# The residual y turned by VectorE instead of TensorE, and the put-off token pieces at fixed groups

## The chip, the cores and the metric

The kernel runs on one core of one Trainium2 chip. The metric is the device time of one execution, in microseconds. All arithmetic is in fp32 (parts of the score factors in an fp32 form with rounded mantissa). The engines are TensorE (PE in the profile, its weight loads PEld), VectorE (DVE), ScalarE (ACT), GpSimd (POOL) and SyncE (SP), which only issues transfers here.

## The reference

Two layers run on x of four images, 64 x 64 positions of 256 channels each, that is 4096 tokens an image.

```python
# layer 0: attention over all 4096 positions of an image
f = xt @ Wf + bf;  g = xt @ Wg + bg;  v = xt @ Wh + bh          # 32, 32, 128 channels
beta = softmax(einsum('bqd,bkd->bqk', g, f))
y = x + (einsum('bqk,bkd->bqd', beta, v) @ Wo + bo)

# layer 1: triangle attention on y, 8 heads of 32 channels
q, k, v1, v2 = (y @ W).reshape(B, N, N, H, d_k)  for each W
att = softmax(einsum('bilhd,bljhd->biljh', q, k) / sqrt(d_k), axis=2)
out = einsum('biljh,bilhd,bljhd->bijhd', att, v1, v2)
h = layer_norm(y + out.reshape(B, N, N, E) @ Wo)
z = relu(h @ W1 + b1) @ W2 + b2 + h
result = layer_norm(z)
```

The change concerns the term y in `layer_norm(y + out @ Wo)`. Layer 0 leaves y with its channels on the partitions; the layer norm needs tokens on the partitions.

## The kernel before

**Stages.** Images b = 0 to 3 go one after the other. Each has an attention stage (`layer0`, line 498) and a triangle stage (`first_layer1` for image 0, `next_layer1`, line 1491, for the others). The token work of layer 1 (projection by Wo, both layer norms, the two-layer perceptron) of image b runs in pieces inside the triangle stage of image b + 1. After image 3's triangle stage its own tokens are left; they run in `alone` (line 1293). A last check over the sums of the softmaxes (`dens`, from line 1634) chooses whether a safe version must run; with these inputs it doesn't.

**Attention stage.** The queries are cut into 8 blocks of 512 tokens (`qb`), the keys into 8 groups (`k`), so that g = 8 qb + k counts 64 groups. In each group `values` (line 569) issues the scores of the next group, the products with v, and on VectorE the running sum of exponentials `esum`. `parts[k]` is a hand-written list of what group k does for the block before: group 0 the normalization (`norm`: a matmul that sums over partitions gives `den`, then a reciprocal on VectorE), group 1 `output` (y = attention x Wo + x, stored to HBM channel by channel), groups 2 to 7 the projections q, k, v1, v2. In group 7 VectorE also folds `esum` into a tile `part` (tag "hid", one buffer). In image 0, VectorE also turns the x of the later images (`ahead.turn`, L356: eight transposes in 32 x 32 blocks and four stores) in every second group. After the last block comes a passage to the triangle stage (from line 776), in which three tiles with tag "R" stage the last block's results, and in which token tile 0 of the image before is begun and the heads of its tile 1 are made.

**Put-off pieces.** In the triangle stages of images 1 and 2 the second layer norm of the tokens is not done; h and z are stored in HBM (`carried_off`, `summed_off`). The attention stage two images later takes them back: for each of 16 tiles `recall` (load), `settle` (three VectorE operations on 512 elements and the statistics), `rooted`, `polished`, `scaled`, `finish` (two GpSimd multiplications or adds, L1287 and L1288, and the store). Line 761 starts a tile every three groups.

**Triangle stage.** Its 32 steps are pairs of heads by 8 rows. In each step the softmax weights are turned by TensorE into `att` (PSUM) and a copy `attP`; eight products R = att x v2 (128 x 2048, L1007) follow, five or six on VectorE and two or three on GpSimd; TensorE sums each R with v1 as stationary data (`accumulate`, L1017). R has three buffers, GpSimd's Rp two. A period is two steps and the pieces of one token tile. The order inside a period is written out as a list of words (`ORDER`, line 43, for images 1 and 2; `ORDER_LAST` for image 3; `ORDER0` for image 0); each engine executes its own share in that order. R, A, T, S, W, V, t, c are work of the steps: product, accumulate, take, row sums and reciprocals, weights, stationary, turn, copy of the weights. sp and e are scores and exponentials; h0 and h1 are the token heads, sa the statistics on them, m the hidden layer, z the output layer, and so on. The number after a slash says how many periods later the word's work is done.

**The line that matters.** `heads` (line 1114) makes out @ Wo for 256 tokens in PSUM with four matmuls (L1120) and adds y by four TensorE transposes (L1125) that accumulate into the same place:

```python
for cc in range(2):
    nc.tensor.matmul(
        hp[:, n, ts(cc, P)], yc[:, cc, ts(n, P)], ident, start=False, stop=(cc == 1),
        is_transpose=True,
    )
```

`yc` is 256 tokens of y, loaded in `load` (line 1095) with one buffer. The statistics on hp are made by `stats_a` on VectorE in the passages and in `alone`, by ScalarE's `sums_of` in the triangle stages of images 1 and 2, and by `stats` on VectorE in image 3's.

Of the kernel before, what the change touches and what calls it, by code (L numbers as in the profile page):

```python
# [10 lines left out]
F32 = mybir.dt.float32  # L11
# [32 lines left out]
    R03/2 R06/2 t1/2 h0 m0/1 R04/2 c1/2 A03/2 A07/2 R16/2 A04/2 A06/2 R12/2 R10/2 T00/2 fi/2 W0/1 sf/2 R17/2  # L44
    T01/2 A10/2 A12/2 t0/1 R11/2 r0/1 fo/2 R13/2 R15/2 f1/2 h1 m1/1 f0/2 A11/2 c0/1 A16/2 V0/1 R14/2 r1/1 A13/2
    A15/2 R00/1 A17/2 T10/2 A14/2 sp/1 R02/1 sa R05/1 e0/1 R01/1 z0/1 rr/1 T11/2 z1/1 pp/1 e1/1 so/1 A00/1 A05/1
    R07/1 W1/1 A02/1 A01/1 fa S1 ht V1/1 S0 hU hT
# [27 lines left out]
def attention_then_triangle_kernel(  # L75
# [131 lines left out]
    dens = ctile([P, NB, 256 + 16], "dens")  # L207
# [238 lines left out]
    class Late:  # L446
# [5 lines left out]
        def load(self, q):  # L452
            self.y = []
            for cc, tag in enumerate(("A", "yc")):
                t = work.tile([P, 512], F32, tag=tag, name="yb", bufs=1)
                nc.sync.dma_start(out=t, in_=self.io["y"][ts(cc, P), ts(q, 512)])
                self.y.append(t)
            self.used = 0
# [39 lines left out]
    def layer0(b, F, safe, rest, ahead):  # L498
# [8 lines left out]
        io["v1"] = dram.tile([T, C], F32, tag="v1", name="v1d")  # L507
        L = Layer1(b, io, safe)
# [105 lines left out]
        def bounds(qb):  # L614
            for j, (t, op) in enumerate(ends.pop(qb)):
                if not safe:
                    c0 = 256 + 2 * qb + j
                    nc.vector.tensor_reduce(dens[:, b, c0 : c0 + 1], t, AX.X, op)
# [7 lines left out]
        def output(qb):  # L626
            col = ts(qb, QB)
            o = oT.pop(qb)
            for cc in range(2):
                y_ps = pb("y")  # L630
                nc.tensor.matmul(y_ps, wo0_sb[:, 0, ts(cc, P)], o, start=True, stop=True)  # L631
                nc.vector.scalar_tensor_tensor(
                    y(qb, cc), y_ps, bo_sb[:, cc : cc + 1], yT[cc][:, col], ALU.add, ALU.add
                )
                nc.sync.dma_start(out=io["y"][ts(cc, P), col], in_=y(qb, cc))

# [91 lines left out]
        if late:  # L728
            parts[3] = [lambda qb: proj(qb, "k", 0)]
            parts[4] = [lambda qb: proj(qb, "v2", 0)]  # L730
            parts[5] = [proj1_half]
            parts[6] = [lambda qb: proj(qb, "q", 1)]
            parts[7] = [lambda qb: proj(qb, "k", 1)]
        last = NQB - 1
        for r in range(4):
            score(0, r)
        for g in range(8 * NQB):
# [22 lines left out]
            if b > 1:  # L760
                for do, late in ((rest.finish, 7), (rest.scaled, 6), (rest.polished, 5), (rest.rooted, 4), (rest.settle, 3), (rest.recall, 0)):
                    if (g - late) % 3 == 0 and 0 <= g - late < 3 * NP:
                        do(NP * (b - 2) + (g - late) // 3)
# [29 lines left out]
        bounds(last)  # L793
        proj(last, "v2", 0, None, stage[1][:, 0, :], nc.scalar)
# [55 lines left out]
    class Layer1:  # L850
        def __init__(self, b, io, safe):
            self.b, self.io, self.safe = b, io, safe

            self.aT = dram.tile([C, 2, N // 2, N], F32, tag="aT", name="aT")
            io["a"] = self.aT
            self.S, self.v2, self.qk, self.v1, self.att, self.ao = {}, {}, {}, {}, {}, {}
            self.R, self.begun, self.acc, self.rec, self.e = {}, {}, {}, {}, {}

# [62 lines left out]
        def sums(self, step):  # L921
# [8 lines left out]
            else:  # L930
                den = dens[:, self.b, ts(step, IG)]
# [111 lines left out]

    class Tokens:
        def __init__(self):
            self.ios = []
            self.A, self.htp = {}, {}
# [47 lines left out]
        def load(self, tt, far=False):  # L1095
# [4 lines left out]
            if far:  # L1100
# [3 lines left out]
                A, yc = both[:, 0].rearrange("p c (i j) -> p c i j", j=N), both[:, 1]  # L1104
            else:
                A = work.tile([P, 2, 4, N], F32, tag="A", name="A", bufs=1)
                yc = work.tile([P, 2, 256], F32, tag="yc", name="yc", bufs=1)
# [3 lines left out]
            nc.sync.dma_start(out=yc, in_=io["y"][:, ts(t, 256)].rearrange("(c p) t -> p c t", p=P))  # L1111
            self.A[tt] = A, yc

        def heads(self, tt, n, psum=pb, new=None):
# [3 lines left out]
            A, yc = self.A[tt]  # L1118
            for cc in range(2):
                nc.tensor.matmul(  # L1120
                    hp[:, n, :], A[:, cc, ts(n, 2), :].rearrange("p i j -> p (i j)"), wo1_sb[:, cc, :],
                    start=(cc == 0), stop=False,
                )
            for cc in range(2):
                nc.tensor.matmul(  # L1125
                    hp[:, n, ts(cc, P)], yc[:, cc, ts(n, P)], ident, start=False, stop=(cc == 1),
                    is_transpose=True,
                )
# [10 lines left out]
        def stats_a(self, tt):  # L1139
            self.stats(self.hps[tt], 0)  # L1140
# [293 lines left out]
    def first_layer1(L, ahead, F):  # L1434
# [29 lines left out]
        for period in range(NSTEP // 4 + 3):  # L1464
            for word, late in words_of(ORDER0):
# [25 lines left out]
    def next_layer1(b, L, rest, ahead, F):  # L1491
# [32 lines left out]
        def of_piece(word, q):  # L1524
# [9 lines left out]
            elif word == "sa" and first:  # L1534
                moments(q - 1)
                if own:
# [55 lines left out]
        for period in range(NP + 4):  # L1592
            for word, late in words_of(ORDER_LAST if own else ORDER):
# [40 lines left out]
    flat = dens.rearrange("p b n -> p (b n)")  # L1634
    nc.vector.tensor_reduce(lim[:, 0:1], flat, AX.X, ALU.min)
    nc.vector.tensor_reduce(lim[:, 1:2], flat, AX.X, ALU.max)
# [42 lines left out]
```

## Time and profile before

| what | value |
|---|---|
| time, median of 3 runs (lowest to highest) | 3630.94 us (3627.85 to 3633.84) |
| the profiled execution's own time | 3633.17 us |
| its span in the profile | 3631.4 us |
| TensorE busy | 3522.3 us (97%) |
| VectorE busy | 2823.5 us (78%) |
| ScalarE busy | 1923.8 us (53%) |
| GpSimd busy | 1779.2 us (49%) |
| transposes of y, L1125 | 256 in two groups (200 and 56), 38.2 + 10.7 us busy |
| products on VectorE, L1007 | 696, 1546.1 us, mean 2279 ns |
| products on GpSimd, L1007 | 328, 1491.4 us, mean 4579 ns |
| token heads, L1120 | 512, 132.4 us |

The stages as the trace shows them, by the first products and the first scores: attention of image 0 to about 440 us; its triangle stage to about 860; attention of image 1 to about 1260, triangle stage to about 1731; image 2 to 2110 and 2592; image 3 to 2990 and 3475; tokens alone to the end. TensorE's records overlap[...]: the mean of one is longer than its place in the queue. What an instruction costs is read from how far apart the starts lie. The profile names a line of the kernel as L and its number.

### The profile page before, as it was taken

The numbers are of one execution on the slowest core, as the hardware profiler recorded it, in microseconds if no ns is written. First come the engines' busy times: TensorE is split into PE (matmuls) and PEld (weight loads), VectorE is DVE, ScalarE is ACT, GpSimd is POOL, SyncE is SP. The second block draws the span as 40 slices with busy tenths as digits, with TensorE's granted clock in tenths as the row PEclk, the third lists the DMA queues.
The fourth block names the chain that finished last, engine by engine and source line by source line (L and its number), as shares of the span: only waits on it lengthen the run. The fifth ranks groups of instructions, "written<-read, shape, count | busy, mean of one in ns | idle before, by whom it ended". The sixth has DMA issues, their size and how long they took to land.

```text
span 3631.4 us, 58644 instructions
## 1 busy us (share of the span) xinstructions
PE 3522.3 (97%) x22282; PEld 1895.3 (52%) x22282; DVE 2823.5 (78%) x2558; ACT 1923.8 (53%) x4221; POOL 1779.2 (49%) x904
## 2 busy tenths in 40 slices
PE   9999999988999999999999999999899999999998
PEld 6555444434555555554455555554455555555477
DVE  4777499996555569999777549999877756999976
ACT  3444455544444366665444446666444436777655
POOL 5000099995000068889211018889611106999920
PEclk9999999999999999999999999999999999999999
DMA  9544555455111354425423254343622235441221
GB/s 174 135 131 127 136 151 137 122 134 136 47 52 52 82 145 108 101 68 107 110 91 95 67 146 109 89 104 76 132 87 95 80 93 134 92 96 46 68 68 55
DMA packets 492594, 370.15 MB, mean 102 GB/s; under 512 B 303184, under 2 KB 434000, under 8 KB 483472
## 3 DMA queue, kind: packets, MB, share of 16 engines
q1 hardware_dynamic: 443264, 339.36, 34.8%
q0 software_dynamic: 36160, 19.94, 5.3%
q10 hardware_dynamic: 12880, 7.01, 0.7%
q8 instruction: 178, 2.92, 0.4%
q14 instruction: 112, 0.92, 0.1%
HBM read 205.73 MB, written 160.43 MB: 101 GB/s over the span
## 4 chain that ended last, share of the span: by engine, by line
PE 67%; POOL 8%; DVE 6%; issue 4%; ACT 1%; DMA 1%; SPq 0%; ACTq 0%; POOLq 0%; DVEq 0%
PE o L579 16%; PE acc L1017 16%; POOL Rp L1007 7%; PE proj L646 6%; PE mp L1253 5%; PE zp L1273 5%; PE s L552 4%; PE sp L905 3%; PE hp L1120 3%; DVE R L1007 2%; PE v1p L678 2%; PE att L959 1%; PE y L631 1%; DVE rec L608 1%; PE htp L1220 1%
## 5 line engine op out<-in xcount | busy, mean ns | idle before, releaser
L1007 POOL TENSOR_TENSOR Rp<-attP,v 128x2048 f32<-128x2048 f32 x328 | 1491.4, 4579 | 409.7 <-ACT attP L967 367.0
L1007 DVE TENSOR_TENSOR R<-att,v 128x2048 f32<-128x2048 f32 x696 | 1546.1, 2279 | 68.6 <-PE acc L1017 49.9
L579 PE MATMUL o<-e,v 128*128 128x512 f32 x2048 | 1043.9, 593 | 0.0
L586 DVE TENSOR_TENSOR esum<-esum,e 128x2048 f32<-128x2048 f32 x224 | 518.8, 2316 | 398.4 <-ACT e L564 395.9
L564 ACT ACTIVATE e<-s 128x1024 f32<-128x1024 f32 x512 | 522.3, 1023 | 529.2 <-PE s L552 438.7
L552 PE MATMUL s<-gT,fT 128*128 128x512 f32 x1024 | 786.7, 770 | 8.7 <-ACT e L564 4.7
L1017 PE MATMUL acc<-R,wsel 128*32 128x512 f32 x5568 | 702.8, 599 | 26.5 <-DVE R L1007 19.6
L579 PEld LDWEIGHTS o<-e,v 128*128 128x128 f32 x2048 | 388.2, 190 | 276.8 <-issue 234.0
L1027 ACT COPY ao<-acc 128x1024 f32<-128x1024 f32 x256 | 256.4, 1013 | 290.4 <-PE acc L1017 205.8
L1017 PE MATMUL acc<-Rp,wsel 128*32 128x512 f32 x2624 | 344.3, 596 | 25.6 <-POOL Rp L1007 23.2
L1017 PEld LDWEIGHTS acc<-R,wsel 128*32 128x32 f32 x5568 | 155.5, 109 | 393.7 <-issue 273.9
L552 PEld LDWEIGHTS s<-gT,fT 128*128 128x128 f32 x1024 | 194.5, 190 | 244.7 <-issue 230.8
L1287 POOL TENSOR_TENSOR hz<-hz,log_bc 128x512 f32<-128x512 f32 x32 | 47.1, 1471 | 542.8 <-ACT hz L1197 474.4
L1181 POOL TENSOR_SCALAR nt<-mv 128x2 f32<-128x2 f32 (+1 forms) x49 | 9.4, 192 | 565.2 <-DVE mv L1137 560.1
L942 ACT ACTIVATE es<-S,rd 128x64 f32<-128x64 f32 x1024 | 258.3, 338 | 15.0 <-DVE rd L934 13.1
L1253 PE MATMUL mp<-hT,w 128*128 128x256 f32 x1024 | 244.4, 384 | 1.7 <-ACT hT L1225 1.7
L1273 PE MATMUL zp<-w,hid 128*128 128x256 f32 x1024 | 239.4, 384 | 0.8 <-ACT hid L1262 0.8
L1253 PEld LDWEIGHTS mp<-hT,w 128*128 128x128 f32 x1024 | 186.5, 190 | 53.0 <-ACT attP L967 12.6
L1273 PEld LDWEIGHTS zp<-w,hid 128*128 128x128 f32 x1024 | 188.0, 190 | 47.8 <-issue 14.7
L608 DVE RECIPROCAL rec<-den 128x512 f32<-128x512 f32 x32 | 107.4, 3357 | 109.7 <-PE den L604 104.4
L1017 PEld LDWEIGHTS acc<-Rp,wsel 128*32 128x32 f32 x2624 | 80.7, 110 | 214.1 <-issue 144.9
L915 ACT ACTIVATE S<-sp 128x512 f32<-128x512 f32 x128 | 131.6, 1094 | 78.0 <-PE sp L905 78.0
(192 smaller groups left out, 3688.4 us busy)
## 6 DMA issues: line engine op xcount, KB each, us to landing
v<-v2d SPq DMA_DIRECT2D x44, 512.0 KB
v1c<-v1d SPq DMA_DIRECT2D x128, 128.0 KB
aT<-ao SPq DMA_DIRECT2D x1024, 16.0 KB
A<-aT SPq DMA_DIRECT2D x256, 64.0 KB
hz<-raw SPq DMA_DIRECT2D x32, 512.0 KB
y<-yT SPq DMA_DIRECT2D x56, 256.0 KB
q<-st SPq DMA_DIRECT2D x56, 256.0 KB
k<-st SPq DMA_DIRECT2D x52, 256.0 KB
```

The source lines that it names most:

```text
L552: nc.tensor.matmul(s_ps[r // 2][:, r % 2, :], fT[tt][:, ts(r * 4 + n, P)], gT[qb // 4][:, ts(qb % 4, QB)], start=True, stop=not safe,)
L564: nc.scalar.activation(e[g][:, 2 * j : 2 * j + 2, :], s_ps[j], AF.Exp)
L579: nc.tensor.matmul(o_ps[qb], F.v[tt][:, r * 4 + n, :], es[:, r, :], start=(k == 0 and r == 0), stop=(k == 7 and r == 3),)
L586: nc.vector.tensor_tensor(esum[qb], esum[qb], es, ALU.add)
L608: nc.vector.reciprocal(rec, den)
L646: nc.tensor.matmul(ps, w[:, cc, rows], y(qb, cc), start=(cc == 0), stop=(cc == 1))
L942: nc.scalar.mul(e[:, i, :], rows[:, i, :], rec[:, i : i + 1])
L1007: eng.tensor_tensor(R, src.unsqueeze(1).to_broadcast([P, D, N]), v2[h], ALU.mult)
L1017: nc.tensor.matmul(acc[32 * c : 32 * c + 32, n % 2, :], w[:, n, c, 16 * h : 16 * h + 32], R[:, ts(c, 8), :].rearrange("p d j -> p (d j)"), ...
L1027: nc.scalar.copy(self.ao[step][:, ts(np, 2)].rearrange("p k d j -> p k (d j)"), self.acc[step][np])
L1253: nc.tensor.matmul(self.mp[:, fc % 2, :], w1_sb[:, cc, ts(fc, P)], self.hT[tt][:, cc, :], start=(cc == 0), stop=(cc == 1),)
L1273: nc.tensor.matmul(zp[:, n, :], self.hid[tt][:, fc, ts(n, P)], w2_sb[:, fc, :], start=(fc == 0), stop=(fc == 3 and tt not in self.hT2),)
```

## The change

1. *A turned copy of y.* In the attention stages of images 0, 1 and 3 (`turned_ahead(b)`: all but image 2), group 5 gets one more part. `turn_y` turns the block of y made before, 512 tokens by 256 channels, by eight VectorE transposes in 32 x 32 blocks, and stores it token by token to a new HBM tensor `yt` with four transfers of 128 KB in runs of 256 bytes. Its tile has tag "hid", one buffer, like `part`. The last block is turned in the passage, in a tile with tag "k8"; its four stores (`L.owed`) are issued at period 1 of the triangle stage.
2. *Heads.* For those images `heads` issues no transposes. `load` brings `yt`, tokens on partitions, and `add_y` adds it to hp with two VectorE adds of 128 x 256 in PSUM, right before the statistics (word "sa", or `stats_a`). Image 2's tokens, which run in image 3's triangle stage, keep the transposes. The tile for y has two buffers.
3. *A new ORDER* for the triangle stages of images 1 and 2. "sa" is its first word. All products of even steps and three of the odd steps' eight come one period late, the other five two periods late; heads are made one period earlier.
4. *Put-off pieces.* Each block of the attention stages of images 2 and 3 takes two tiles t = 0, 1, at fixed groups: recall at t, settle at 3 + t, rooted at 4 + t, polished at 5 + t, scaled at 6 + t, and both finish at 7.
5. *Sums of the softmaxes.* `dens` is kept for one image; `limits(b)` reduces it to a smallest and a largest value for each image, at group 1 of the next attention stage, and for image 3 at the end.

```diff
 ORDER = """
-    R03/2 R06/2 t1/2 h0 m0/1 R04/2 c1/2 A03/2 A07/2 R16/2 A04/2 A06/2 R12/2 R10/2 T00/2 fi/2 W0/1 sf/2 R17/2
-    T01/2 A10/2 A12/2 t0/1 R11/2 r0/1 fo/2 R13/2 R15/2 f1/2 h1 m1/1 f0/2 A11/2 c0/1 A16/2 V0/1 R14/2 r1/1 A13/2
-    A15/2 R00/1 A17/2 T10/2 A14/2 sp/1 R02/1 sa R05/1 e0/1 R01/1 z0/1 rr/1 T11/2 z1/1 pp/1 e1/1 so/1 A00/1 A05/1
-    R07/1 W1/1 A02/1 A01/1 fa S1 ht V1/1 S0 hU hT
+    sa R11/2 A13/2 A10/2 A11/2 T01/2 R12/2 sp/1 r0/1 e0/1 e1/1 t0/1 m1/1 R14/2 A12/2 A17/2 fo A14/2 R00/1 V0/1
+    R16/2 T10/2 r1/1 A16/2 c0/1 S1/1 W1/1 rr/1 R07/1 R15/2 A00/1 A15/2 z1/1 R01/1 T11/2 z0/1 pp/1 t1/1 R03/1
+    A01/1 R02/1 so/1 fa A07/1 A03/1 c1/1 R06/1 A02/1 ht hT S0 hU T00/1 fi/1 R05/1 h1/-1 V1/1 h0/-1 m0 R04/1
+    R13/1 W0 sf/1 R10/1 A04/1 A06/1 A05/1 f0/1 R17/1 f1/1
 """.split()
...
+    dens = ctile([P, 256 + 16], "dens")
+    lims = ctile([P, 2, NB], "lims")
+    def limits(b):
+        for j, op in enumerate((ALU.min, ALU.max)):
+            nc.vector.tensor_reduce(lims[:, j, b : b + 1], dens, AX.X, op)
...
+        def turn_y(qb, **where):
+            t = work.tile([P, 16, 2, 32], F32, name="yr", **where)
+            for cc in range(2):
+                rows = y(qb, cc).rearrange("p (k t) -> p k t", t=32)
+                for k in range(4):
+                    nc.vector.transpose(t[:, ts(k, 4), cc, :], rows[:, ts(k, 4), :])
+            def kept():
+                for r in range(4):
+                    nc.sync.dma_start(
+                        out=io["yt"][ts(qb, QB), ts(r, 64)].rearrange("(k t) c -> t k c", t=32),
+                        in_=t[ts(r, 32)].rearrange("t k h c -> t k (h c)"),
+                    )
+            return kept
...
+        if turned_ahead(b):
+            parts[5].append(lambda qb: turn_y(qb, tag="hid", bufs=1)())
...
             if b > 1:
-                for do, late in ((rest.finish, 7), (rest.scaled, 6), (rest.polished, 5), (rest.rooted, 4), (rest.settle, 3), (rest.recall, 0)):
-                    if (g - late) % 3 == 0 and 0 <= g - late < 3 * NP:
-                        do(NP * (b - 2) + (g - late) // 3)
+                for t in range(2):
+                    for do, at in (
+                        (rest.recall, t), (rest.settle, 3 + t), (rest.rooted, 4 + t), (rest.polished, 5 + t),
+                        (rest.scaled, 6 + t), (rest.finish, 7),
+                    ):
+                        if k == at:
+                            do(NP * (b - 2) + 2 * qb + t)
+            if g == 1 and b > 0 and not safe:
+                limits(b - 1)
...
         bounds(last)
+        if turned_ahead(b):
+            L.owed = turn_y(last, tag="k8")
...
-            nc.sync.dma_start(out=yc, in_=io["y"][:, ts(t, 256)].rearrange("(c p) t -> p c t", p=P))
-            self.A[tt] = A, yc
+            src = io["yt"][ts(t, 256)] if turned_ahead(b) else io["y"][:, ts(t, 256)]
+            nc.sync.dma_start(out=yt, in_=src.rearrange("(n p) c -> p n c", p=P))
+            self.A[tt], self.yt[tt] = A, yt
...
-                    start=(cc == 0), stop=False,
-                )
-            for cc in range(2):
-                nc.tensor.matmul(
-                    hp[:, n, ts(cc, P)], yc[:, cc, ts(n, P)], ident, start=False, stop=(cc == 1),
-                    is_transpose=True,
-                )
+                    start=(cc == 0), stop=(cc == 1 and turned_ahead(tt // NP)),
+                )
+            if not turned_ahead(tt // NP):
+                for cc in range(2):
+                    nc.tensor.matmul(
+                        hp[:, n, ts(cc, P)], self.yt[tt][:, cc, ts(n, P)], ident, start=False, stop=(cc == 1),
+                        is_transpose=True,
+                    )
+
+        def add_y(self, tt):
+            hp, yt = self.hps[tt], self.yt.pop(tt)
+            if not turned_ahead(tt // NP):
+                return
+            for n in range(2):
+                own = hp[:, n, :].rearrange("p (h r c) -> p h r c", h=2, r=4)
+                nc.vector.tensor_tensor(own, own, yt[:, n, :].rearrange("p (r h c) -> p h r c", h=2, r=4), ALU.add)
...
         def stats_a(self, tt):
+            self.add_y(tt)
             self.stats(self.hps[tt], 0)
...
         for period in range(NP + 4):
+            if period == 1:
+                L.owed()
```

## The prediction on record

> **What bounds the kernel now.** I read the busy time by stretches first. Its columns are the stretch, its length, and for each engine busy us with the count of instructions, then the clock, DMA share and GB/s. The first two rows are single periods of the triangle stage of image 1, the last is a period near its end.
>
> ```profile
> core 0: us, PE busy (x) PEld busy (x) DVE busy (x) ACT busy (x) POOL busy (x), PEclk, DMA share, GB/s
> 1359.10:1386.21 27.11, 27.11 (x250) 14.52 (x249) 26.04 (x16) 17.93 (x51) 24.11 (x12) 1.00 0.22 59
> 1386.21:1413.31 27.10, 27.10 (x249) 14.50 (x249) 25.91 (x16) 17.91 (x51) 24.09 (x12) 1.00 0.61 142
> 1655.00:1682.20 27.20, 25.85 (x188) 13.09 (x187) 26.30 (x16) 16.78 (x50) 26.63 (x17) 1.00 0.56 105
> ```
>
> Here TensorE sets the pace: busy for 27.10 of 27.10 us. But VectorE is busy 26.0 of them: it has only 1.1 us to give. Near the end, when no scores are left for TensorE, VectorE and GpSimd pace it at 27.20.
>
> Next, the timeline of TensorE in the second of those periods shows what a transpose of y costs there.
>
> ```profile
> 1394.29 1.03 PE L1120 MATMUL hp<-wo,A 128*128 128x256 f32 x4
> 1395.15 0.38 PE L1125 MATMUL hp<-ident,yc 128*128 128x128 f32 x2
> 1395.37 1.91 PE L1253 MATMUL mp<-hT,w 128*128 128x256 f32 x8
> ```
>
> [...] starts are what count. The two transposes move the next start by 0.22 us (1395.15 to 1395.37), not by 0.38. Four to a tile are 0.43 us (0.22 + 0.21 for the other pair).
>
> VectorE's row of the same period:
>
> ```profile
> 1389.53 0.69 DVE L932 TENSOR_REDUCE dens<-S 128x8 f32<-128x512 f32 x1 [0.57 <-ACT S L915]
> 1390.24 0.20 DVE L934 RECIPROCAL rd<-dens 128x8 f32<-128x8 f32 x1
> 1390.37 0.63 DVE L932 TENSOR_REDUCE dens<-S 128x8 f32<-128x512 f32 x1
> ...
> 1398.35 15.51 DVE L1007 TENSOR_TENSOR R<-att,v 128x2048 f32<-128x2048 f32 x7 [0.56 <-PE acc L1017]
> ```
>
> Seven products take 15.51 us, 2.216 each; two row sums with their reciprocals take 1.62 (1389.53 to the product at 1391.15). Eleven products and two sums: 11 x 2.216 + 1.62 = 26.0.
>
> Then the start of that stage, on TensorE and VectorE:
>
> ```profile
> 1299.81 6.69 DVE L1007 TENSOR_TENSOR R<-att,v 128x2048 f32<-128x2048 f32 x3 [3.91 <-ACT attP L967]
> ...
> 1302.74 0.38 PE L1125 MATMUL hp<-ident,yc 128*128 128x128 f32 x2
> 1302.96 3.62 PE L1273 MATMUL zp<-w,hid 128*128 128x256 f32 x16
> ```
>
> The first product starts at 1299.81, 3.15 us ahead of the end of tile 1's heads. That head start is what the new order touches.
>
> [...]
>
> ```profile
> 3619.51 0.42 DVE L1343 TENSOR_TENSOR z<-zp,z 128x256 f32<-128x256 f32 x1
> ```
>
> [...] The trace shows an esum of 3.33 us at 1766.98, where 2.29 is usual, beside the put-off tile's multiplications on GpSimd.
>
> **The change, part by part.** The sum is made against the profiled execution: 3633.17 us, span 3631.4. The median of the runs, 3630.94, is 2.2 lower, so I take a difference from the former to the latter.
>
> *Triangle stages of images 1 and 2 (tokens of images 0 and 1, the ones turned ahead).* TensorE loses 0.43 us a period: 27.10 - 0.43 = 26.67. VectorE gains two adds, the second waiting for the first. The adds L1352, L1353 of this shape start 0.46 apart (3622.98, 3623.44), so the pair is 0.46 + 0.39 = 0.85 us[...]. VectorE: 26.0 + 0.85 = 26.85. So VectorE becomes the bound, 0.18 us above TensorE, and of 0.43 us at most 0.25 can be kept.
>
> Now the whole stage on VectorE. Before: first product 1299.81, last ends at 1730.10, 430.3 us; work in it 176 products x 2.216 = 390.0 and 30 sums x 0.81 = 24.3; 16.0 idle. After: in the new order "sa" stands first, so the adds for tile 1 are queued ahead of the first product, and wait for tile 1's heads, which TensorE ends at 1302.96 less 0.43 = 1302.5. Behind them on VectorE waits the whole stage: first product, then the first sum of step 1 (now after it). Start: +2.7. Work: 390.0 + 31 x 0.81 = 25.1, + 15 tiles x 0.85 = 12.8, together 427.9. Idle: four late periods, paced by GpSimd at 27.20, leave 27.20 - 26.85 = 0.35 each, 1.4; twelve steady ones, with two engines within 0.2 us and three R buffers between them, somewhere from 0 to the 1.1 of now, I take 0.25, 3.0; the first period 1.5. Sum 2.7 + 427.9 + 5.9 = 436.5, against 430.3: **+6.2 us, twice: +12.4**. Bounds: with no idle +0.3 each; with today's 16.0, +16.3 each. What follows the adds (ScalarE's sums over hp, roots, GpSimd's polish, the affine) has until the turn of h late in the period, some 20 us; I see no wait there. ScalarE is busy 17.9 of 27.1.
>
> *Attention stages: turning y.* Eight transposes a block; the same instruction on x takes 2.02 us for eight (L356). VectorE is busy 26 of 50 us in image 1's attention, TensorE 50.00 of 50. In image 0's, VectorE has 36.8 of 50, and still waits 3.5 us a block for den (24.4 in 7). So I cost them at nothing; without that cover they would cost up to 2.0 us a block. The tile shares its single buffer with "part", which two groups later must wait until the four stores have landed. Four such stores of x take 1.9 to 2.2 us to issue on SyncE; between transposes and part lie about 10 us. Cover, unless landing takes over 7 us; GpSimd's issues of 256 KB land in 6.8 to 7.6, so this is not sure. Bounds: 0, or 1 us a block in 21 blocks. I take 0. The stores stand on SyncE's queue between v1 and the next q; those have a group of 5 to 6 us. The last block's eight transposes fall in a VectorE gap of 20.75 us (1273.4 to 1294.2); its stores are issued in the triangle stage's period 1, among 16 smaller ones: nothing.
>
> *Put-off pieces.* In images 2 and 3 the wait list shows what the old places cost:
>
> ```profile
> PE proj L646 <- DVE yT L632: 1.9, 2, 1.0
> PE y L631 <- DVE oT L610: 0.3, 1, 0.3
> ```
>
> The same 1.9 and 0.3 stand in image 3. New places keep the long step ("settle", 3.3 us) at groups 3 and 4, off the heavy groups 7, 0 and 1: -4.4. But both tiles of a block finish on GpSimd in group 7, also in the last block, where TensorE waits for esum at once; one lengthening of 1.04 us (3.33 - 2.29) in each image gives back 2.1. In other blocks the wait for den (23.5 us in 6) hides it. Net -2.3. The ends: -4.4 and +2.
>
> *Tokens alone (image 3).* A tile takes 9.51 us (outputs start 3534.07, then 3543.58). TensorE would need 9.08. But from the end of heads (3533.79) over stats, roots, residue, finish, sums, roots to the last hid (3542.85) are 9.1 us on VectorE and ScalarE without a gap to spare, and the adds make it 9.95. From outputs to the next heads' end are 9.18 - 0.43 = 8.75. Both loops close over two tiles: (9.95 + 8.75 + 0.05)/2 = 9.37. Gain 0.14 x 13 tiles = -1.8. Ends: 0, and 0.43 x 13 = -5.6.
>
> *Limits.* Two reductions over 1088 elements, 1.27 us each, leave VectorE's busy tail of the last triangle stage (49.59 of 50); two over 272 come, about 0.43 each (0.68 for 512 at L618, less 240 elements), and two tiny ones of 0.15: -1.4. There also the two first tiles of image 3 take adds, the second 0.85 near the end: together -0.5. The other limits, 0.9 us, lie in attention groups with idle VectorE: nothing.
>
> Sum: 12.4 - 2.3 - 1.8 - 0.5 = **+7.8 us**. 3633.2 + 7.8 = 3641.0 profiled, and 2.2 less, 3639, as a median.
>
> **Rivals.**
> (1) *VectorE is bound, with little idle* (mine): 3632 to 3646. For it: 26.85 above 26.67, and the queued adds. Chance 0.58.
> (2) *The order locks.* Both engines are within 1% of the period, so each late accumulation holds one of three R buffers. If idle stays at today's 16.0 a stage: 10.1 more than mine, twice: 3659. For it: the waits of VectorE on acc are 11.7 us in the twelve steady periods already. Against: those came from a saturated TensorE, which now has slack. The store of turned blocks holding "part" gives the same sign. Chance 0.24.
> (3) *Not slower: TensorE's relief is kept.* VectorE idles nowhere (+0.3 each instead of +6.2: -11.8) and the alone stage keeps its 0.43 (-3.8): 3639 - 15.6 = 3623. It decides where the pair of adds costs under 0.7 us and idle under 1 us in a stage. For it: TensorE's 27.10 of 27.10. Against: the start, whose 2.7 us nothing repays. Chance 0.18.
> (4) That the change does not do what it says is excluded: the order of the built kernel has no transposes of y left on TensorE for images 0, 1 and 3, and has the adds ahead of the first product.
>
> **How the numbers follow.** About 0.2%, 7 us, is what a measurement of this kernel can tell from none; so "same" is 3623.7 to 3638.2. Case 1 puts 0.32 above and 0.26 inside; case 2 0.20 above and 0.04 inside; case 3 0.11 below and 0.07 inside. Faster 0.11, same 0.37, slower 0.52. The range 3624 to 3654 leaves 0.1 below and 0.1 above.
>
> **What would show it.** Steady periods of 26.9 to 27.1 us with VectorE above 99% and TensorE below; the first product of that stage at 2.7 us or more after the end of the old one, with the adds ahead of it waiting for heads; tiles of 9.3 to 9.4 us alone; no wait of proj on yT in images 2 and 3. I am wrong if periods come to 26.7, or above 27.3, if attention stages lengthen by part's wait on DMA, or if adds take 0.6 us a pair.

## The result, and the profile after

The changed kernel takes 3647.41 us (median of 6 runs, 3645.83 to 3653.72) beside 3631.31 us for the kernel before (6 runs, 3627.85 to 3634.52): ratio 1.0046, 95% interval 1.0033 to 1.0059. It is slower by 16.1 us, where 7.8 were forecast. The profiled execution is the slowest of the six (3653.72 us, span 3651.9), so its trace shows 20.5 us against the other trace.

Where do they lie? I take one mark for each stage: the first score on TensorE for an attention stage, the first product on VectorE for a triangle stage. The stretch up to a triangle stage's mark holds the passage too.

```
stretch              before    after   difference
to the first score    42.37    43.74     +1.4
attention 0          401.22   404.08     +2.9
triangle 0           428.34   435.59     +7.3
attention 1          427.88   431.40     +3.5
triangle 1           431.61   431.71     +0.1
attention 2          431.10   435.34     +4.2
triangle 2           431.61   433.31     +1.7
attention 3          431.18   434.34     +3.2
triangle 3, alone    606.09   602.39     -3.7
```

Of the 6.2 us that the forecast gave each of the two stages, 3.55 (the late start and the first pair of adds) lie before the first product, and so in the rows of attention 1 and 2; these came. The other 2.6 belong to the rows of triangle 1 and 2, which move by 0.1 and 1.7 (in the runs below that keep this order and a single pair of adds, they stand at 431.1 to 431.8, once at 433.0). Single executions differ by some us in places that no edit touches (the end of triangle 0 above all, see below), so a row counts here only where other kernels repeat it.

First the periods of triangle 1 after, as busy time by stretches with the columns of the prediction.

```profile
core 0: us, PE busy (x) PEld busy (x) DVE busy (x) ACT busy (x) POOL busy (x), PEclk, DMA share, GB/s
1385.80:1412.60 26.80, 26.70 (x245) 14.12 (x244) 26.53 (x18) 18.05 (x53) 24.16 (x13) 1.00 0.57 119
1412.60:1439.40 26.80, 26.72 (x245) 14.13 (x244) 26.55 (x18) 18.07 (x53) 24.15 (x13) 1.00 0.62 147
```

A period is 26.80 us, where 26.85 was forecast. But VectorE, forecast as the bound, is busy 26.55 of it and TensorE 26.72. Both are so near that busy time cannot say which of them sets the pace.

Next the start of that stage, VectorE's timeline. Brackets give how long the engine stood idle before a row, and what ended it.

```profile
1305.38 0.69 DVE L966 TENSOR_REDUCE dens<-S 128x8 f32<-128x512 f32 x1 [18.24 <-ACT S L949]
...
1313.97 0.90 DVE L1176 TENSOR_TENSOR hp<-hp,yt 128x256 f32<-128x256 f32 x2 [7.66 <-PE hp L1159]
1314.81 2.29 DVE L1041 TENSOR_TENSOR R<-att,v 128x2048 f32<-128x2048 f32 x1
```

VectorE stands still for 7.66 us until TensorE has made the heads, adds y, and only then starts the first product. The pair moves the next start by 0.84 us (0.85 in the prediction).

Then the start of triangle 0, which the prediction didn't treat. SyncE's timeline, VectorE's first product there, and TensorE's scores behind it:

```profile
404.72 2.59 SPq L654 DMA_DIRECT2D yt<-yr  x4
407.55 1.29 SPq L901 DMA_DIRECT2D q<-q  x2
...
415.39 14.50 SPq L922 DMA_DIRECT2D v<-v2d  x4
...
447.13 2.46 SPq L907 DMA_DIRECT2D k<-k  x4
```

```profile
447.82 6.69 DVE L1041 TENSOR_TENSOR R<-att,v 128x2048 f32<-128x2048 f32 x3 [5.63 <-DMA v<-v2d]
```

```profile
454.50 2.61 PE L939 MATMUL sp<-q,k 32*64 32x64 f32 x64 [5.91 <-DMA k<-k]
```

In the kernel before:

```profile
409.59 5.34 SPq L888 DMA_DIRECT2D v<-v2d  x4
...
438.02 9.67 SPq L873 DMA_DIRECT2D k<-k  x4
```

```profile
443.59 6.69 DVE L1007 TENSOR_TENSOR R<-att,v 128x2048 f32<-128x2048 f32 x3 [2.94 <-ACT attP L967]
```

```profile
446.97 2.04 PE L905 MATMUL sp<-q,k 32*64 32x64 f32 x64
```

The four stores of a turned block stand ahead of the loads for the triangle stage. The loads of v2 begin at 415.39 and take 14.50 us to be issued; before, they begin at 409.59 and take 5.34. The first product waits 5.63 us for them; before it waited 2.94, for attP. The delay runs on in the queue: the next loads of k start at 447.13 in place of 438.02, and the scores wait 5.91 us for them, where they waited for no load before. Counted from the first score, these scores start 6.2 us late (410.8 beside 404.6), about what the run e4 below gives as the cost of this queue.

In the attention stage of image 3, the two largest entries of TensorE's wait list are these (what waited, for what; us in total, times, longest):

```profile
PE den L613 <- DVE esum L598: 3.1, 1, 3.1
PE proj L669 <- DVE stage L639: 1.7, 1, 1.7
```

The waits on yT (1.9 us) are gone as forecast, and these have come: the first was 1.2 us in the kernel before, the second is new.

In the stage `alone`, two outputs in a row on TensorE's timeline:

```profile
3555.28 3.70 PE L1322 MATMUL zp<-w,hid 128*128 128x256 f32 x16
...
3564.48 3.70 PE L1322 MATMUL zp<-w,hid 128*128 128x256 f32 x16
```

A tile takes 9.20 us here and 9.07 in four earlier ones; 9.51 before, 9.37 forecast.

### The profile page after: what moved, and what is told of

Its sections match the earlier page's. It is cut to its first block, busy times and chain, and to the rows that moved or that the text cites. A ratio compares the mean times of both kernels' runs of the same rounds, so it can differ in the third digit from the quotient of the medians.

```text
span 3651.9 us, 58627 instructions
## 1 busy us (share of the span) xinstructions
PE 3505.2 (96%) x22090; PEld 1877.1 (51%) x22090; DVE 2916.1 (80%) x2854; ACT 1927.9 (53%) x4221; POOL 1778.2 (49%) x904
## 4 chain that ended last, share of the span: by engine, by line
PE 63%; POOL 17%; DVE 8%; issue 6%; ACT 3%; DMA 2%; SPq 0%; ACTq 0%; POOLq 0%; DVEq 0%
PE o L586 23%; POOL Rp L1041 15%; PE acc L1051 10%; PE proj L669 8%; PE s L559 6%; DVE R L1041 4%; PE mp L1302 3%; PE sp L939 3%; PE v1p L701 2%; PE zp L1322 2%; PE y L638 2%; PE hp L1159 1%; PE att L993 1%; ACT hid L1311 1%; PE v1p L439 1%
```

## The experiments

The theory after the traces: the adds' wait at the start of triangles 1 and 2, the stores on SyncE's queue before triangle 0, and the pieces' last block cost; the alone stage gains. The rival was the one of the forecast, that the order of the period or VectorE as the bound takes the time. Each kernel is compared with runs of the kernel before on its own chip.

```
run              median    before    ratio   95% interval
changed kernel   3647.41   3631.31   1.0046  1.0033 to 1.0059
e1_pieces        3644.35   3630.61   1.0035  1.0021 to 1.0049
e2_order         3710.34   3630.61   1.0215  1.0201 to 1.0229
e3_first_sa      3638.25   3630.61   1.0020  1.0013 to 1.0026
e4_queue         3640.66   3630.61   1.0027  1.0018 to 1.0036
e5_two           3631.25   3632.76   0.9995  0.9989 to 1.0002
e6_three         3628.41   3632.76   0.9989  0.9983 to 0.9996
e7_image3        3629.55   3632.76   0.9991  0.9985 to 0.9998
e8_new_order     3637.61   3632.76   1.0009  1.0001 to 1.0018
e9_no_add        3628.47   3631.57   0.9994  0.9987 to 1.0001
e10_add_twice    3660.58   3631.57   1.0078  1.0062 to 1.0095
e11_last_block   3631.83   3631.57   0.9998  0.9989 to 1.0006
e12_old_add      3637.76   3631.57   1.0020  1.0013 to 1.0026
```

**The first tile's adds behind the first product.**

```diff
+ORDER_1 = [w for v in ORDER[1:] for w in ((v, "sa") if v == "R00/1" else (v,))]
...
-            for word, late in words_of(ORDER_LAST if own else ORDER):
+            for word, late in words_of(ORDER_LAST if own else ORDER_1 if period == 1 else ORDER):
```

> The changed kernel with one word moved in one period: in the first period of the triangle stages of images 1 and 2 the first tile's adds and sums stand after the first product, in all other periods where the change puts them. If the wait of the first add for the heads holds back the whole stage, the first product comes 2.7 us earlier in both stages and all after it too: 5 us less, 3641 to 3643. The rival is that GpSimd, which paces the last periods, or TensorE takes the gain back before the stage ends: within 1 us of the changed kernel, 3646 to 3648.

The excess over the kernel before falls from 16.1 to 7.6 us. In the trace, attention 1 with its passage is 427.64 us long (431.40 in the changed kernel), attention 2 431.59 (435.34): 3.75 us each. Triangle 1, 431.30 long, gives none of it back. VectorE at the start of triangle 1:

```profile
1304.23 2.29 DVE L1042 TENSOR_TENSOR R<-att,v 128x2048 f32<-128x2048 f32 x1 [4.70 <-ACT attP L1002]
1307.14 0.90 DVE L1177 TENSOR_TENSOR hp<-hp,yt 128x256 f32<-128x256 f32 x2 [0.62 <-PE hp L1160]
```

The product fills the time in which the heads are made; the adds wait 0.62 us instead of 7.66. The rival, that the late periods take it back, falls. The gain in medians is larger than expected, 8.5 instead of 5 us; 7.5 of it are the two starts, and the last us is not placed.

**The stores before triangle 0 on another queue.**

```diff
+            queue = nc.gpsimd if b == 0 and qb == last - 1 else nc.sync
             def kept():
                 for r in range(4):
-                    nc.sync.dma_start(
+                    queue.dma_start(
```

> The changed kernel with the four stores of the turned block before the last in image 0 issued on GpSimd's queue instead of SyncE's; the same bytes in the same runs of 256 bytes. If the loads of v2 for the first products of image 0's triangle stage are late because SyncE's queue stands behind these stores, the wait of the first product on v2 (5.6 us) goes, and the time falls by 4 to 7 us: 3640 to 3643. If the DMA engines' work is what counts, or the late loads belong to the one execution that was profiled, the time stays within 1.5 us of 3647.4.

6.1 us come back in the excess (16.1 to 10.1). SyncE's timeline:

```profile
409.42 5.65 SPq L923 DMA_DIRECT2D v<-v2d  x4
417.68 10.14 SPq L373 DMA_DIRECT2D xT<-ahx  x4
```

The same loads begin 6.0 us earlier (4.4 counted from the first score) and are issued in 5.65 us, about as in the kernel before. The first product waits 2.94 us, as long as in the kernel before, no longer 5.63 us for v2, and the fourth row sum of triangle 0 comes 7.0 us earlier, counted from the first score. This repeats: that row sum stands 415.5 to 418.0 us behind the first score in the five kernels below and above that keep these stores on SyncE's queue, with a wait of the first product of 4.1 to 5.6 us, and 409.6 to 411.3 us, with a wait of 2.94, in all others, the kernel before among them. The bytes and their runs of 256 bytes are the same, and the loads are issued in 5.65 us instead of 14.50, so the DMA engines' work alone is not the cause. But GpSimd's queue also issues the four stores 4.7 us earlier (counted alike), while on SyncE's they follow a store of v1 that is issued at 404.27; whether the other queue or the earlier time helps was not separated. In the changed kernel's trace SyncE stands still for 10.6 us before the third of these loads; its own wait list puts that down to the landing of a store of q (`q<-stage`). In the kernel before, the list has no wait of these loads longer than 3.6 us (for `k<-k`). Why the loads come to wait for that landing is not shown. Whether the number of packets or the bytes ahead of the loads makes the delay was not tried.

**Both edits.** Both diffs together.

> The changed kernel with two edits together: the first tile's adds stand after the first product in the first period of the two triangle stages, and image 0's four stores of the block before the last go on GpSimd's queue. Alone the first left 7.6 us above the kernel before and the second 10.1, of 16.1. If the two delays are separate ones, they add: 16.1 - 8.5 - 6.0 = 1.6 us above the kernel before, about 3632 (3629 to 3635). If both removed the same thing (a shift of where a stage's transfers fall), the second brings nothing more: 3637 to 3640.

The two are separate delays: the time is that of the kernel before within the measurement (0.9995). In medians the two edits take 17.6 us off the excess, where the sum of the two alone is 14.5. About 3 us between these figures stay unexplained. One source of such differences is seen in the traces: at the end of triangle 0 TensorE waits for a load of x, 2.3 us in one execution (e6), 6.6 in another (e5) and 4.9 in that of the kernel before, although no edit touches it.

**The put-off pieces.** In the changed kernel, and with the two edits:

```diff
-                for t in range(2):
-                    for do, at in (
-                        (rest.recall, t), (rest.settle, 3 + t), (rest.rooted, 4 + t), (rest.polished, 5 + t),
-                        (rest.scaled, 6 + t), (rest.finish, 7),
-                    ):
-                        if k == at:
-                            do(NP * (b - 2) + 2 * qb + t)
+                for do, late in ((rest.finish, 7), (rest.scaled, 6), (rest.polished, 5), (rest.rooted, 4), (rest.settle, 3), (rest.recall, 0)):
+                    if (g - late) % 3 == 0 and 0 <= g - late < 3 * NP:
+                        do(NP * (b - 2) + (g - late) // 3)
```

> The changed kernel with the put-off pieces back at one tile every three groups. The prediction had the new places as a gain of 2.3 us (4.4 us of stalls gone, 2.1 us of lengthened sums in the last blocks), so by it this kernel is 2.3 us slower than the changed one: about 3649.7. The trace of the changed kernel shows more than the 2.1 us at the ends of the attention stages of images 2 and 3 (TensorE waits 3.1 us there for the folds of esum, 1.2 before, and 1.7 us more in image 3 for the store of a put-off tile). If these are the pieces' doing, the new places gain nothing or lose up to 2.5 us: this kernel at 3645 to 3648, with the waits of proj on yT (1.9 us) and of y on oT (0.3) back in images 2 and 3.

> As the kernel with the two edits, and the put-off pieces back at one tile every three groups, which alone took 2.4 us. If the three are separate, 0.8 us under the kernel before: 3630 (3627 to 3632), and the end of image 3's attention stage has no wait of TensorE for the store of a put-off tile. If the pieces' cost was chance, the same as the kernel with two edits.

The old places are 2.4 us better in the one and 2.8 in the other. The intervals of each pair overlap, but the traces place it. Attention 3 is 431.25 and 431.22 us long with the old places, as in the kernel before (431.18), and 434.34 and 433.45 with the new. Attention 2 is the same with both (e6 431.49, e5 431.54), because two effects cancel. From the first score to the last block's first fold of `esum` the new places take 390.7 us in both images, the old ones 392.4: 1.7 us of the forecast 2.2 an image came, as the waits on yT went. From that fold to the stage tile the new places take 10.6 us in image 2 and 12.5 in image 3 (e5), the old ones 8.6 in both (e6): 2.0 and 3.9 us lost. VectorE at the end of image 3's attention, first in e6, then in the changed kernel:

```profile
2981.35 1.22 DVE L597 TENSOR_TENSOR esum<-esum 128x1024 f32<-128x1024 f32 x1
2982.61 0.69 DVE L599 TENSOR_TENSOR esum<-esum 128x512 f32<-128x512 f32 x1
...
2989.95 1.54 DVE L640 SCALAR_TENSOR_TENSOR stage<-y,bo_sb,yT 128x512 f32<-128x512 f32 x2 [1.29 <-PE y L639]
```

```profile
3003.58 2.29 DVE L593 TENSOR_TENSOR esum<-esum,e 128x2048 f32<-128x2048 f32 x1 [2.75 <-ACT e L571]
3005.91 2.17 DVE L596 TENSOR_TENSOR esum<-esum 128x1024 f32<-128x1024 f32 x1
3008.11 1.63 DVE L598 TENSOR_TENSOR esum<-esum 128x512 f32<-128x512 f32 x1
...
3019.26 1.41 DVE L639 SCALAR_TENSOR_TENSOR stage<-y,bo_sb,yT 128x512 f32<-128x512 f32 x2 [3.20 <-DMA out_dram<-hz]
```

```profile
3004.61 2.40 POOL L1336 TENSOR_TENSOR hz<-hz,log_bc 128x512 f32<-128x512 f32 x1 [39.98 <-ACT hz L1246]
3007.08 2.12 POOL L1337 TENSOR_TENSOR hz<-hz,lob_bc 128x512 f32<-128x512 f32 x1
```

In the changed kernel GpSimd finishes two tiles from 3004.61 on (the last two lines), one multiplication taking 2.40 us. The folds lengthen by 1.9 us together, and the stage tile waits 3.20 us for the store of a put-off tile, since both use the tag "R". From VectorE's end at 3005.87 on they end in turn: GpSimd 1.14 us later, VectorE 1.07 after that, GpSimd 1.12 and VectorE 0.54, where undisturbed such instructions take 1.27, 1.22, 1.27 and 0.69. What holds each of them while the other engine works is not shown.

A first mend was to do the last block's steps one group earlier (e5 with this edit):

```diff
-                        (rest.recall, t), (rest.settle, 3 + t), (rest.rooted, 4 + t), (rest.polished, 5 + t),
-                        (rest.scaled, 6 + t), (rest.finish, 7),
+                        (rest.recall, t), (rest.settle, 3 + t - early), (rest.rooted, 4 + t - early),
+                        (rest.polished, 5 + t - early), (rest.scaled, 6 + t - early), (rest.finish, 7 - early),
```

Here `early` is 1 in the last block, and 0 else.

> The kernel with the two edits, and in the last block of images 2 and 3 all steps of the two put-off tiles but their loads one group earlier, so that both finish in group 6. If the finish in group 7 is what lengthens the folds of esum (TensorE's wait 3.1 us, of which 1.2 stood before) and, in image 3, holds the buffer of the passage's stage, then about 2.5 us go, in image 3 above all, and the time is 3628 to 3629.5. If the loss comes from the other blocks, the time stays at 3631.

Nothing is gained. The trace shows why: GpSimd's work on the second tile (2981.90 to 2986.50) still lies on both folds, and the stage tile waits 4.29 us for the store, longer than in the changed kernel.

```profile
2983.21 2.17 DVE L597 TENSOR_TENSOR esum<-esum 128x1024 f32<-128x1024 f32 x1
2985.41 1.63 DVE L599 TENSOR_TENSOR esum<-esum 128x512 f32<-128x512 f32 x1
...
2996.70 1.41 DVE L640 SCALAR_TENSOR_TENSOR stage<-y,bo_sb,yT 128x512 f32<-128x512 f32 x2 [4.29 <-DMA out_dram<-hz]
```

One group was too little; two were not tried. The run does not separate the folds from the other blocks, which it was meant to do; the stretches of e5 and e6 above do.

**Image 3 alone.** `turned_ahead(b)` returns `b == NB - 1`, with the old order and the old places of the pieces.

> Only image 3's y is turned ahead, whose tokens run alone after the last triangle stage; images 0, 1 and 2 keep TensorE's transposes, the old order and the old places of the pieces. In the alone stage the changed kernel's tiles took 9.1 to 9.2 us instead of 9.51, 3.7 us in all with the last triangle stage. If this gain is the change's only one, this kernel keeps it and nothing else: 3.7 us under the kernel before, about 3627. If turning y costs in image 3's attention stage, where VectorE has also the put-off pieces, what is left is less: 3629 to 3631.

It is 3.2 us faster than the kernel before: the last stretch is 602.13 us (606.09). Attention 3 is 431.23, so turning y there costs nothing that shows.

**The new order without adds.** The kernel before, with only the table `ORDER` exchanged.

> The kernel before with the new order of words alone: TensorE's transposes of y, no adds. The old order with the adds cost 63 us more than the new one with them, so the new order is what carries the adds; the question is what it does without them. If the place of the adds at the head of the period, and not the order, was the loss at the start of the stage, then without adds VectorE is held by nothing there and TensorE sets the period at 27.1 us: within 3 us of the kernel before, 3628 to 3634. If the order itself delays the stage, its two stages are 3 us or more longer each: 3636 to 3645.

Neither fits wholly: 4.9 us in medians, 3.3 by the ratio. Attention 1 is 427.65 us, so without adds the start is not held. But triangles 1 and 2 are 433.5 us each, 1.9 more than in the old order. The steady periods are 26.95 us, shorter than the 27.11 of before; the last ones, where no scores are left, take 27.6 and 27.8 in place of 25.8 and 26.8. With adds the same order mostly gives 431.1 to 431.8: relief of TensorE brings 2.2 us a stage there, and the order takes nearly all of it.

**The old order with the adds.** The changed kernel with the table `ORDER` of before.

> The changed kernel with the old order of words in the triangle stages of images 1 and 2; the adds stay, and stand after three products instead of ahead of all. If the new order's place for the adds is what costs (they hold the first product back until the heads are made), this is 4 to 6 us faster than the changed kernel, 3641 to 3643, with steady periods of 26.8 to 26.9 us. The rival, that the old order leaves too little slack between heads, adds and products once VectorE is the bound, expects periods of 27.2 us or more and 5 to 15 us more: 3652 to 3662.

Each of the two stages is 34 us longer (465.8). The rival was right in its direction and far too small: 3662 was its upper end. The wait lists of ScalarE and TensorE over four periods:

```profile
ACT junk L1200 <- DVE hp L1176: 19.8, 4, 5.0
```

```profile
PE acc L1051 <- ACT ao L1061: 7.4, 4, 1.9
```

TensorE ends the second half of the heads at 1419.2, but the adds run at 1428.75, behind products. ScalarE's sums stand 5.0 us a period on the adds, its copies of acc stand behind these sums, TensorE's accumulation waits for the copies (7.4 us in four waits), and VectorE's products for the accumulation (5.8 us in six waits between 1400 and 1508): a lock in a ring.

**The old order, adds two products ahead.** A word of its own for the adds, shown against the kernel of the last experiment:

```diff
-    A15/2 R00/1 A17/2 T10/2 A14/2 sp/1 R02/1 sa R05/1 e0/1 R01/1 z0/1 rr/1 T11/2 z1/1 pp/1 e1/1 so/1 A00/1 A05/1
+    A15/2 ad R00/1 A17/2 T10/2 A14/2 sp/1 R02/1 sa R05/1 e0/1 R01/1 z0/1 rr/1 T11/2 z1/1 pp/1 e1/1 so/1 A00/1 A05/1
...
+            elif word == "ad" and first:
+                rest.add_y(tt)
             elif word == "sa" and first:
                 moments(q - 1)
-                rest.add_y(tt)
                 if own:
+                    rest.add_y(tt)
```

> The changed kernel with the old order (which was 63 us slower than the changed kernel), and in it only VectorE's adds moved two products ahead, in front of the first step's first product; ScalarE's sums over the heads stay where they are. In the old order ScalarE waited 5.0 us in every period for the adds, which stood behind products, and its copies of acc stood behind that. If this wait makes the 34 us of each stage, it goes with the move, and the time is 3645 to 3665. If the old order lacks slack in general, less than a third of the 63 us comes back: over 3690.

The whole 63 us go, and 10 more: 73 us, the medians taken against the kernel before. What is left is 6.2 us over the kernel before, where the changed kernel is 16.1 over.

```profile
ACT junk L1200 <- DVE hp L1176: 2.8, 5, 0.6
```

Periods are 26.89 us, and from its first product triangle 1 takes 426.7 us, 4.6 less than in e3, of which 3.8 only come from the later first product; its late periods are 26.55 us, while the new order's grow to 27.4 and 27.7. The first adds wait 6.9 us for the heads here also, and the stretch to the first product is again 431.4 us. From the first score of image 1 to that of image 2 it is 858.1 us with this order, 858.9 in e3, 859.5 before and 863.1 in the changed kernel.

**Without adds, and with each twice.** Both on e5's kernel.

```diff
-                nc.vector.tensor_tensor(own, own, yt[:, n, :].rearrange("p (r h c) -> p h r c", h=2, r=4), ALU.add)
+                for _ in range(2):
+                    nc.vector.tensor_tensor(own, own, yt[:, n, :].rearrange("p (r h c) -> p h r c", h=2, r=4), ALU.add)
```

The other kernel leaves the line out, so that y is missing from the sum.

> The kernel with the two edits (first tile's adds behind the first product, image 0's four stores on GpSimd's queue), without the adds: y is loaded but left out of the sum for images 0, 1 and 3, so that VectorE has 0.85 us a tile less. If VectorE at 26.80 us is the bound of the periods and TensorE at 26.67 the next, periods come to 26.67, and each of the two triangle stages is 1 to 2 us shorter; the alone tiles, where TensorE's own work is 9.07 us, hardly change: 3627 to 3629.5 against 3631.3. If GpSimd or the R buffers pace the periods, nothing changes: 3631.

> The same kernel with every pair of adds made twice, so that y counts double in images 0, 1 and 3. If VectorE is the bound, a period is 26.80 + 0.85 = 27.65 us, the two triangle stages 15 x 0.85 = 12.8 us longer each, and the alone tiles, whose chain over VectorE was 9.2 us, 0.85 longer, 14 tiles 12: together 37 us, 3668. If the adds stand in gaps of VectorE, less than half of that: under 3650.

Without adds the period doesn't move. VectorE's row sums of one kind, from one period to the next, and between them its waits:

```profile
1377.58 0.68 DVE L968 TENSOR_REDUCE dens<-S 128x8 f32<-128x512 f32 x1
...
1394.91 2.29 DVE L1043 TENSOR_TENSOR R<-att,v 128x2048 f32<-128x2048 f32 x1 [0.29 <-PE acc L1053]
1397.76 6.68 DVE L1043 TENSOR_TENSOR R<-att,v 128x2048 f32<-128x2048 f32 x3 [0.56 <-PE acc L1053]
1404.37 0.68 DVE L968 TENSOR_REDUCE dens<-S 128x8 f32<-128x512 f32 x1
```

It is 26.79 us with 0.84 us less on VectorE, which now waits 0.85 us for TensorE instead. So VectorE is not the bound of the changed kernel, although the period was forecast to 0.05 us. The total, 3628.47, lies in the range that was expected of a bound VectorE, but not for that reason: the two triangle stages are only 0.5 and 0.8 us shorter than in e5, and the alone tiles take 9.07 us throughout, where the later ones take 9.2 with adds. With two pairs a period is 27.48 us:

```profile
1382.55 0.67 DVE L968 TENSOR_REDUCE dens<-S 128x8 f32<-128x512 f32 x1
...
1399.51 1.82 DVE L1179 TENSOR_TENSOR hp<-hp,yt 128x256 f32<-128x256 f32 x4
1410.03 0.67 DVE L968 TENSOR_REDUCE dens<-S 128x8 f32<-128x512 f32 x1
```

Now VectorE is the bound, with no wait in the period, and 27.48 - 0.85 = 26.6 is what it needs with one pair: 0.2 us under the period. A triangle stage grows by 9.1 us (440.2 beside 431.1), not 12.8; an alone tile from 9.2 to 10.1 us. The total, 3660.6, lies under the 3668 expected.

What sets 26.80 then? TensorE's timeline without adds (e9), and in the new order with transposes (e8), at the same place of the period:

```profile
1393.77 1.07 PE L1053 MATMUL acc<-R,wsel 128*32 128x512 f32 x8
1394.66 2.18 PE L1053 MATMUL acc<-Rp,wsel 128*32 128x512 f32 x16
1396.65 2.76 PE L1053 MATMUL acc<-R,wsel 128*32 128x512 f32 x24
```

```profile
1399.77 1.06 PE L1017 MATMUL acc<-R,wsel 128*32 128x512 f32 x8
1400.66 1.90 PE L1017 MATMUL acc<-Rp,wsel 128*32 128x512 f32 x16
1402.37 2.76 PE L1017 MATMUL acc<-R,wsel 128*32 128x512 f32 x24
```

Sixteen matmuls on GpSimd's products move the next start by 1.71 us in e8 and by 1.99 in e9: 0.28 us of waiting between them. That is what is left of the relief: 26.95 - 0.43 + 0.28 = 26.80. The changed kernel has the same row (2.21 us, next start 2.02 later). The weight loads' wait list names a product of GpSimd there (Rp, 6.0 us in six periods; 3.2 in e8). GpSimd itself waits 11.4 us in these six periods of e9 for copies of the weights (attP), so it is not full; the place of the words in the order may make this wait as well as GpSimd's speed. No run took GpSimd's work away, so the cause of the 0.28 us is not shown.

## Why the prediction was partly right

The sign and the range held, with "slower" as the likeliest outcome. But the sum, 7.8 us, was half of what was measured, 3647.41 lies above the 3632 to 3646 of the prediction's own likeliest case, and several terms were wrong in cause or in size. That the total stayed in the range is in part luck: a cost of 5.3 us that did not come (the rest of the two stages) stands against one of 6 that was put at nothing (the queue). Of the signs named, the late start and the end of the waits on yT came; periods of 26.9 us or more with VectorE busier than TensorE, and tiles of 9.3 us alone, did not.

- *The start of triangles 1 and 2.* Right. The prediction had +2.7 and the first pair's 0.85, 3.55 in all; e3 shows 3.75 us each, not given back.
- *"So VectorE becomes the bound."* This step failed. The period was forecast at 26.85 and measured at 26.80, but it is so without adds too. VectorE needs 26.6: I had divided a row's whole length by its products (2.216 us each), where starts count; in e9 four products move the next start by 8.75 us, 2.19 each. TensorE, forecast to need 26.67 us, needs 26.52 in the new order (26.95 - 0.43) and loses 0.28 us waiting inside its period.
- *The rest of the stage, +2.6 each.* Mis-sized. Measured from the first product it is 0.1 us in triangle 1: e8's order loss of 1.9 and TensorE's relief of about 2.2 cancel.
- *Turning y and its stores, 0.* On VectorE right: attention 1 is 427.63 us with the turn (e5) and 427.60 without (e7), attention 0 401.17 and 401.36. As for the stores the step failed. I looked at SyncE's queue in ordinary blocks ("a group of 5 to 6 us") and for the landing, not at the last block, where the triangle stage's first loads follow in the same queue. About 6 us, by e4; what of it is the queue and what the time of issue stays open.
- *Put-off pieces, -2.3.* Failed; it is about +2.5. The gain was near the forecast, 1.7 us an image instead of 2.2. The last block's price was mis-sized: it was taken from one lengthening of 1.04 us, where two folds lengthen by 1.9 and in image 3 the stage waits for a store, so that 2.0 us are lost in image 2 and 3.9 in image 3 (e5 beside e6).
- *Alone and limits, -1.8 and -0.5.* Too small: -4.0 together (e7, 602.13 beside 606.09). I let a chain through VectorE and ScalarE set the tile; TensorE's own 9.08, which the text had named, was what early tiles took (9.07), and all of them without adds (e9). The adds cost about 0.12 us in the later ones.
- *The rivals.* That the order locks is real, but for the old order with adds, not for the order that was built. That TensorE's relief is kept needed a stage start without loss; e5 has that and comes only to the time of before, since the order takes the relief.

The changed kernel's excess is thus made of the two starts (7.5), the queue (6), the pieces (2.5), less the alone stage (4.0); the rest, about 4 us of 16, was not placed. It goes with the three edits, which leave e6 at 4.4 us under the kernel before, but no run tells with which. Since the alone stage makes 4.0 of these 4.4, the turn of y for images 0 and 1 has brought next to nothing. The fastest kernel that was run is e6, the change with all three edits: 0.9989 of the kernel before, interval 0.9983 to 0.9996, close to e7 (0.9991), which turns only image 3. The old order with the adds moved, with the start and the queue mended too, might be better; it was not tried.

## What to carry to other kernels

When work goes to another engine, look first at who stands in line behind it at the ends of a stage: an add ahead of the first product, or a store ahead of the first loads, cost more here (7.5 and about 6 us) than all steady periods of the two stages gained (0.31 us each, some 22 of them). A period that comes out as forecast does not show that the forecast bound is the bound; double the work and leave it out, and see which of the two moves it. In an order written by hand, a wait of one engine for another is a matter of place: the same adds, two products ahead, were worth 73 us.

## What was not expected of the hardware

With four stores of 128 KB in runs of 256 bytes ahead on SyncE's queue, four later loads of v2 took 14.50 us to issue instead of 5.34, the third issued 11.5 us after the second; with the stores issued on GpSimd's queue, and 4.7 us earlier, the loads took 5.65. A fold of 128 x 1024 on VectorE took 2.17 us beside GpSimd's multiplication and 1.22 without, while the multiplication took 2.40 us beside it and 1.27 where VectorE was free; the two engines' instructions ended in turn, 1.14, 1.07, 1.12 and 0.54 us apart.
